# Second-half scores directly behind the first half's sums, and weight forms on another engine, in a two-layer graph network

## The chip, the cores and the metric

The kernel runs on one core of one Trainium2 chip. The metric is the device time of one execution in microseconds (us). The kernel before takes 2780.09 us (median of 3 runs, 2779.88 to 2780.28); the profiled execution below has a span of 2778.7 us. The engines are named as in the profile: PE is TensorE's matmul row and PEld its weight loads, DVE is VectorE, ACT is ScalarE, POOL is GpSimd, SP is the queue that issues most transfers.

## The reference, cut to what matters

Input x holds 128 graphs of 128 nodes with 256 features, adj their 0/1 adjacency. All is float32. Two layers run one after the other, each graph by itself:

```python
# layer 0: attention over the graph's nodes, 8 heads of 32
q, k = heads(src @ Wq + bq), heads(src @ Wk + bk)
attn = softmax(einsum('bhid,bhjd->bhij', q, k) / sqrt(dh))     # over all nodes
for r in range(4):
    v_r = heads(src @ Wv[r] + bv[r])
    out += einsum('bhij,bhjd->bhid', attn * (adj == r), v_r)
x = ln(src + out @ Wo + bo);  x = ln(x + gelu(x @ W1 + b1) @ W2 + b2)
# layer 1: two graph-attention steps, then a feed-forward
h = gat(gat(x, adj, W1, a1), adj, W2, a2)
x = ln(x + h);  x = ln(x + relu(x @ w_ff1 + b) @ w_ff2 + b)
```

adj is 0 or 1, so of the four values v_r only two are ever used. The kernel computes attn on v_0 and the masked attn on v_1 - v_0, adds both, and divides by the plain row sums of the exponentials. A slower pass for other inputs stands behind a test at the end; it does not run here.

## The kernel before, in words

**Tiling.** The 16384 nodes go through in 32 groups of four graphs, 512 rows each (`G = 4`, `T = 512`). A group passes through projections, attention (`attention`), norm, first feed-forward (`first_ffn`), norm, the graph-attention layer (`layer1`), norm, second feed-forward (`second_ffn`), norm and store. Work of three to four groups is woven together.

**Seven products for eight.** The large matrix products are cut into 2 by 2 blocks and done with seven block products instead of eight. That needs sums and differences of the weight blocks, the forms T1 to T4, made once by `combined` (line 182) with four subtractions each for the weights w1, w2 (first feed-forward), wqk, wv (projections), u1, u2 (second feed-forward). On GpSimd these are 24 instructions. It also needs sums of the input blocks, `yS` and `xS`, made by VectorE for every group. A feed-forward (`ffn`, line 394) runs two rounds of the first matrix. In a round, the products into the banks pa (tag "fa"), pe (tag "fe") and `seeded` (tag "fb") follow one another in this order: B11 into pa, which ScalarE copies to `seeded` (line 449 or 483); T3 into pe, copied out to p7; T2 added into `seeded`, copied out to p16; B21 into pa; T1 into `seeded`; T4 into pe; B22 into `seeded`. Each feed-forward block is two products with a 128 by 256 result, which the trace shows as four matmuls. Then come seven products with the second matrix (`product2`, line 420).

**Attention.** A group's four graphs are handled in two halves p = 0, 1 of two graphs. `scores` (line 693) multiplies keys and queries with four 32-row tiles of the array side by side, into four banks (`ps`), and ScalarE takes the exponentials into e. `masked` multiplies e by adj (VectorE, line 725), giving pm. `sums` (line 730) multiplies e and pm by the values into `pav` with four 32-column tiles side by side, and e by ones into `pden`: the plain sums. In groups after the second the plain sums follow pav. ScalarE then reads pden twice (lines 764 and 767: a copy to rd with a running sum, and a relu for the test at the end), VectorE takes the reciprocal and multiplies. `output` projects by Wo.

**Banks.** There are eight: two of tag "s", shared by the transposes, graph-attention products, scores and plain sums, and one each of "qa", "qb", "av", "fa", "fe", "fb". The tile pools make a later user of a bank wait for the readers of the earlier one.

**Order.** The order is written out by hand. Every stage is a generator; `in_order` takes (generator, number of steps) pairs and emits the steps in that order, each engine in its own queue and first in, first out. Step names in the lists: `f1`, `f2` the two feed-forwards, `at` attention, `pr` projections, `l1` the graph-attention layer, `n0` to `n3` the norms, `turned` the transposes of a group with the input sums, `ahead` the same for the second feed-forward's input, `gelu` and `exp` ScalarE's table switches. In the steady loop the second half's scores come four feed-forward blocks behind the first half's sums:

```python
f2, at, (f2, 2), n1, at, f2, at, (f2, 2), lambda: turned(S1, 1), f2, at, (n2, 2), (f2, 2),
```

Here the three first `at` are the first reciprocal, the second reciprocal with the product, and the whole of the second scores.

Of the kernel before, what the change touches and what calls it, by code (L numbers as in the profile page):

```python
# [10 lines left out]
F32 = mybir.dt.float32  # L11
# [13 lines left out]
P = 128  # L25
# [82 lines left out]
def fast_pass(ctx, tc, a, out):  # L108
# [5 lines left out]
    nc = tc.nc  # L114
# [3 lines left out]
    NCH = D // P  # L118
# [14 lines left out]
    ps_s = ctx.enter_context(tc.tile_pool(name="ps_s", bufs=2, space=PSUM))  # L133
    ps_1 = ctx.enter_context(tc.tile_pool(name="ps_1", bufs=1, space=PSUM))
# [46 lines left out]

    def combined(w):
        for o, p, q in ((T3, B22, T1), (T1, T1, B11), (T2, B22, T1), (T4, B21, T2)):
            nc.gpsimd.tensor_sub(w[:, o], w[:, p], w[:, q])


    temp = flat(w1p.tile([P, NF, T], F32, tag="hT", name="temp"))
# [10 lines left out]
    first = dict(g=0, direct=0, xt=load_xT(0))  # L198
    wqk = halved("qk", lambda h: a["L0_gnn_W" + "qk"[h]])
# [3 lines left out]
    wv = halved("v", lambda h: a["L0_gnn_Wv"][h])  # L203
# [14 lines left out]
    w1, b1 = forms("L0_gnn_W1"), k.col("L0_gnn_b1")  # L218
# [4 lines left out]
    w2 = forms("L0_gnn_W2")  # L223
# [469 lines left out]
    def scores(S, p):  # L693

        qT, kT = S["qT"], S["kT"]
        n = f"{S['g']}_{p}"


        banks = ((ps_1, "qa"), (ps_1, "qb"), (ps_s, "s"), (ps_s, "s"))
        pss = [  # L700
            pool.tile([P, 2, NCH, P], F32, tag=t, name=f"ps_{n}_{s}")
            for s, (pool, t) in enumerate(banks if p == 0 and S["g"] > 1 else banks[2:] + banks[:2])
        ]
        for u in range(2):
            bs = slice((2 * p + u) * P, (2 * p + u + 1) * P)
            for c in range(NCH):
                for s in range(HC):
                    rs = slice(s * DH, (s + 1) * DH)
                    nc.tensor.matmul(  # L709
                        pss[s][:, u, c, :], kT[rs, c, bs], qT[rs, c, bs],  # L710
                        start=True, stop=True,
                    )
        S["e", p] = e = w1p.tile([P, HC, 2, NCH, P], F32, tag="e", name="e_" + n)
        for s in range(HC):
            nc.scalar.activation(e[:, s], pss[s], AF.Exp, scale=SCALE)  # L715
            if s == 1:
                yield
# [12 lines left out]
    def sums(S, p):  # L730


        e, pm = S["e", p], S["pm", p]
        n = f"{S['g']}_{p}"
        pden = ps_s.tile([P, 2, NCH, P], F32, tag="s", name="pden_" + n)
        pav = ps_1.tile([P, 2, NCH, P], F32, tag="av", name="pav_" + n)

        def plain():
            for s in range(HC):
                nc.tensor.matmul(  # L740
                    pden[s * DH : (s + 1) * DH], k.ones, e[:, s], start=True, stop=True
                )


        late = S["g"] > 1
        if not late:
            plain()
        for u in range(2):
            v = S["v"][:, 2 * p + u]
            for c in range(NCH):  # L750
                for r, m in enumerate((e, pm)):
                    for s in range(HC):
                        d0 = r * D + c * P + s * DH
                        nc.tensor.matmul(  # L754
                            pav[s * DH : (s + 1) * DH, u, c, :],
                            v[:, d0 : d0 + DH], m[:, s, u, c, :],
                            start=(r == 0), stop=(r == 1),
                        )
        if late:
            plain()  # L760

        g, oT = S["g"], S["oT"]
        rd = w1p.tile([P, 2, NCH, P], F32, tag="rd", name="rd_" + n)
        nc.scalar.activation(
            rd, pden, AF.Identity, accum_out=c_att[:, 1, g, p : p + 1]
        )
        nc.scalar.activation(
            pden, pden, AF.Relu, bias=k.lo, scale=-1.0, accum_out=c_att[:, 0, g, p : p + 1]
        )
        yield  # L770
        nc.vector.reciprocal(rd[:, 0], rd[:, 0])
        yield
        nc.vector.reciprocal(rd[:, 1], rd[:, 1])
        for u in range(2):
            bs = slice((2 * p + u) * P, (2 * p + u + 1) * P)
            nc.vector.tensor_mul(oT[:, :, bs], pav[:, u], rd[:, u])
        yield

    def attention(S):

        n = str(S["g"])
        S["oT"] = oT = w1p.tile([P, NCH, T], F32, tag="oT", name="oT_" + n)

        def output(p):
            po = mm_tile(f"pwo_{n}_{p}")
            for s in range(2):
                b = 2 * p + s
                for c in range(NCH):
                    nc.tensor.matmul(  # L789
                        po[:, s * D : (s + 1) * D], oT[:, c, b * P : (b + 1) * P], wo[:, c, :],  # L790
                        start=(c == 0), stop=(c == NCH - 1),
                    )
            added(S, 0, p, po)

        for p in range(G // 2):
            parts = scores(S, p)
            next(parts)
            if p == 0:
                yield
            next(parts, None)  # L800
            yield
            masked(S, p)
            yield
            yield from sums(S, p)
        for p in range(G // 2):
            output(p)
            yield
# [116 lines left out]
    with tc.manual_schedule(engines={ET.PE, ET.Activation, ET.DVE, ET.SP, ET.Pool}):  # L924
# [6 lines left out]
        S1 = st[1]  # L931
# [4 lines left out]
        def output_bias():  # L936
# [7 lines left out]
            prepared(first)  # L944

        in_order(
            lambda: combined(w1), (pr, 4), (at, 2), (pr, 2), at, (pr, 2), at, lambda: combined(w2), (at, 3), (pr1, 2),
            at, output_bias, at, (pr1, 2), (at, 3), pr1, at, (at1, 2), n0, n0, pr1, at1, lambda: turned(first, 0), (at1, 2),
        )
        f1 = first_ffn(first)  # L950
        prepared(S1)
        st[2] = entered(2)
        pr = projected(st[2])
        in_order(
            gelu, (f1, 4), pr1, f1, f1, at1, at1, f1, pr1, lambda: combined(wqk), lambda: combined(wv), lambda: combined(u1), f1, n0, at1, (f1, 2), n0, f1, at1,
            (f1, 3), gwu, at1, f1, gwu, f1, at1, gwu,
            f1, at1, f1, gwu, at1, lambda: combined(u2), f1, n0_, pr, n0_, (f1, 4), n1_, (pr, 5), lambda: turned(S1, 0),
        )
        for g in range(NG - 1):
            S, S1 = st[g], st[g + 1]  # L960
            more = g + 2 < NG
            f1, f2 = first_ffn(S1), second_ffn(S)
            n1, n2 = norm(S1, 1), norm(S, 2)
            at = n0 = none
            if more:
                S2 = st[g + 2]
                at, n0 = attention(S2), norm(S2, 0)
            ahead = lambda: turned(S, 2)
            ready = (lambda: prepared(st[g + 2])) if more else (lambda: None)
            if g == 0:  # L970
                l1 = layer1(S)
                in_order(
                    f1, n1_, (pr, 2), (f1, 3), lambda: turned(S, 1), (pr, 2), f1, (n0_, 2), f1, l1, f1, (n1_, 2), l1, l1, f1, l1,
                    (f1, 2), (l1, 2), (pr, 2), f1, l1, (pr, 2), f1, pr, l1, f1, l1, f1, (l1, 2), exp, f1, (at, 2), (l1, 2),
                )
            else:
                n3 = norm(st[g - 1], 3)
                in_order(
                    pr, lambda: turned(S1, 0), (pr, 2), *(() if more else (f2_,)), f1, l1, gelu, (pr, 2), f2_, n3, f1, l1, pr,
                    n0_, f1, (pr, 2), (f1, 3), n0_, l1, f1, (pr, 2), l1, f1, n3, (pr, 2), f1, l1, f1, n3, (pr, 2),  # L980
                    (f1, 3), n3, lambda: store(st[g - 1]), f1, (n1_, 2), exp, (at, 2), f1, (l1, 3),
                )
            in_order(
                f1, (pr, 2), l1, f1, (pr, 2), at, f1, (pr, 2), l1, n2, (pr, 2), f1, n2, (pr, 2), f1, (pr, 2), f1, (pr, 2), *((ahead,) if more else ()), at, f1, n1,
                *(() if more else (ahead,)),
            )
            if not more:
                break
            l1 = layer1(S1)
            pr = none  # L990
            if g + 3 < NG:
                st[g + 3] = entered(g + 3)
                pr = projected(st[g + 3])
            in_order(
                f2, at, (f2, 2), n1, at, f2, at, (f2, 2), lambda: turned(S1, 1), f2, at, (n2, 2), (f2, 2),
                at, f2, l1, ready, (f2, 3), l1, f2, at, f2, l1, (f2, 2), at, at, f2, at, n0, l1, f2,
                n0, l1, pr, f2, *((f2,) if g + 3 < NG else ()),
            )
            n0_, n1_, f2_ = n0, n1, f2
        in_order(f2, n1, (f2, 2), lambda: turned(S1, 1))  # L1000
        l1 = layer1(S1)
        in_order(
            (f2, 2), (l1, 3), f2, l1, (f2, 2), (l1, 2), n1, (f2, 2), l1, n1, (f2, 2), (l1, 2), f2, l1, n2, f2, (l1, 3), n2,
            (f2, 3), l1, (f2, 2), l1,
        )
        n2, n3 = norm(S1, 2), norm(S, 3)
# [361 lines left out]
```

## Time and profile before

| what | value |
|---|---|
| time, median of 3 | 2780.09 us |
| period of a group in the steady part (1328.60 to 1412.89) | 84.29 us |
| PE busy from 396 to 1418 us | 1019.6 of 1022 us |
| PE busy from 0 to 140 us | 119.4 of 140 us |
| PE busy from 2660 to 2779 us | 96.2 of 119 us |
| POOL, forms (line 184), start | 24 subtractions: 16 of 1.6 us, 8 of 0.73 us (medians) |
| DVE mask multiply 128x512, median of 256, longest | 0.682 us, 1.765 us |
| mean granted PE clock, 70 to 140 us and 2740 to 2779 us | 0.93 and 0.85 of full speed, about 1.00 elsewhere |

How to read it: in a timeline line the first number is the start in us from the span's start, the second how long the group of instructions lasted, then engine, line, operation, output and inputs, array rows and columns used, shape and how many. A square bracket at the end gives the idle time of the engine before it and what released it. Matmul ends are modelled; the distance from one start to the next, the pitch, is the firm number. In the list of waits the columns are engine and line, what was waited for, total us, how often, and the longest. A PE that is busy 98% of the span leaves 53 us of holes; what a change can close is read in the stage where the hole is.

### The profile page before, as it was taken

The page shows a single profiled execution, that of the slowest core. Times are in us where ns is not written, and L with a number is a line of the kernel's source. Part 1 is how long each engine was busy: PE and PEld are TensorE (multiplying, and loading weights), DVE is VectorE, ACT ScalarE, POOL GpSimd, SP SyncE. Part 2 cuts the span into 40 slices and gives each one's busy share as a digit, 9 for nine tenths or more (in the row PEclk, how much of TensorE's full clock was granted, in tenths as well). Part 3 has the DMA queues.
Part 4 walks back from the last instruction along what each step waited for, and adds up shares of the span by engine and source line. Part 5 has one row for each costly group of instructions (what it writes and reads, how often), then busy time and mean ns, then how long its engine had stood idle before and what let it go on. Part 6 is the DMA issues. An engine that isn't in the chain of part 4 may idle for free.

```text
span 2778.7 us, 54158 instructions
## 1 busy us (share of the span) xinstructions
PE 2725.9 (98%) x21621; PEld 2372.0 (85%) x21621; DVE 2287.3 (82%) x5296; ACT 1613.9 (58%) x3589; POOL 166.7 (6%) x161
## 2 busy tenths in 40 slices
PE   8899999999999999999999999999999999999997
PEld 5688888888888888888888888888888888888876
DVE  5778888888888888888888888888888888888876
ACT  4456556556565566565565565565655665655653
POOL 2200000000000000000000000000000000000000
PEclk9999999999999999999999999999999999999999
DMA  6001100010100101000101000111001110001000
GB/s 177 1 24 32 35 16 28 32 35 32 35 16 24 35 32 35 24 28 24 35 32 35 16 30 29 35 31 35 17 24 35 32 35 27 25 24 35 13 12 17
DMA packets 70234, 86.12 MB, mean 31 GB/s; under 512 B 8428, under 2 KB 48728, under 8 KB 69976
## 3 DMA queue, kind: packets, MB, share of 16 engines
q1 hardware_dynamic: 68872, 82.20, 9.5%
q8 instruction: 172, 2.82, 0.4%
q14 instruction: 86, 0.70, 0.1%
q10 hardware_dynamic: 1104, 0.40, 0.1%
HBM read 65.68 MB, written 16.90 MB: 30 GB/s over the span
## 4 chain that ended last, share of the span: by engine, by line
PE 89%; ACT 4%; DVE 3%; issue 3%; DMA 1%; SPq 0%; ACTq 0%; POOL 0%; DVEq 0%; POOLq 0%
PE po L420 16%; PE ph L411 13%; PE seeded L411 13%; PE seeded L420 12%; PE pqqa L641 4%; PE pwo L789 4%; PE pw L862 4%; PE pvqa L641 4%; PE pav L754 3%; PE pt L300 3%; PE pvqb L641 3%; PE pqqb L641 3%; PE ps L709 2%; PE py L875 2%; PE pg L888 2%
## 5 line engine op out<-in xcount | busy, mean ns | idle before, releaser
L349 ACT ACTIVATE x<-x,sh,rs 128x256 f32<-128x256 f32 x388 | 201.4, 590 | 424.3 <-DVE sh L344 424.3
L335 POOL TENSOR_TENSOR rs<-rs,mhalf 128x4 f32<-128x4 f32 x129 | 133.4, 1034 | 2554.3 <-DVE rs L334 2310.6
L466 DVE TENSOR_TENSOR hT<-seeded,p 128x512 f32<-128x512 f32 x128 | 88.5, 691 | 156.0 <-ACT hT L435 89.5
L411 PE MATMUL seeded<-yS,w_L_gnn_w_ff 128*128 128x256 f32 x768 | 207.3, 392 | 4.9 <-ACT seeded L483 2.2
L411 PE MATMUL seeded<-yS,w_L_gnn_W 128*128 128x256 f32 x768 | 202.0, 386 | 3.2 <-ACT seeded L483 2.2
L411 PE MATMUL ph<-yT,w_L_gnn_w_ff 128*128 128x256 f32 x768 | 200.9, 385 | 0.9 <-ACT yT L303 0.9
L411 PE MATMUL ph<-yT,w_L_gnn_W 128*128 128x256 f32 x768 | 197.4, 379 | 0.4 <-ACT yT L303 0.4
L320 DVE BATCH_NORM_STATS2 st<-x 128x6 f32<-128x256 f32 x512 | 192.1, 417 | 6.7
L411 PEld LDWEIGHTS seeded<-yS,w_L_gnn_w_ff 128*128 128x128 f32 x768 | 138.1, 190 | 63.1 <-ACT seeded L483 28.1
L420 PE MATMUL po<-w_L_gnn_W,hT 128*128 128x128 f32 x1536 | 190.0, 277 | 0.0
L420 PEld LDWEIGHTS po<-w_L_gnn_W,hT 128*128 128x128 f32 x1536 | 183.9, 192 | 6.8
L420 PE MATMUL po<-w_L_gnn_w_ff,hT 128*128 128x128 f32 x1536 | 187.0, 275 | 0.0
L420 PEld LDWEIGHTS po<-w_L_gnn_w_ff,hT 128*128 128x128 f32 x1536 | 184.1, 192 | 3.3
L411 PEld LDWEIGHTS ph<-yT,w_L_gnn_w_ff 128*128 128x128 f32 x768 | 141.1, 190 | 43.3 <-issue 25.2
L411 PEld LDWEIGHTS seeded<-yS,w_L_gnn_W 128*128 128x128 f32 x768 | 138.5, 190 | 40.6 <-DVE hT L466 12.1
L725 DVE TENSOR_TENSOR pm<-e,adj 128x512 f32<-128x512 f32 x256 | 170.2, 725 | 0.0
L411 PEld LDWEIGHTS ph<-yT,w_L_gnn_W 128*128 128x128 f32 x768 | 145.6, 190 | 20.8 <-ACT yT L303 0.7
L435 ACT ACTIVATE hT<-hT,c_L_gnn_b 128x256 f32<-128x256 f32 x256 | 109.5, 497 | 60.2 <-DVE hT L466 58.5
L715 ACT ACTIVATE e<-ps 128x512 f32<-128x512 f32 x256 | 129.8, 589 | 7.5 <-PE ps L709 7.4
L435 ACT ACTIVATE hT<-hT,c_L_gnn_b_ff 128x256 f32<-128x256 f32 x256 | 110.1, 514 | 33.9 <-DVE hT L466 29.6
L834 ACT ACTIVATE gs<-spread,wh 128x128 f32<-128x128 f32 x120 | 38.4, 390 | 156.9 <-DMA spread<-hbm 156.9
L420 PEld LDWEIGHTS seeded<-w_L_gnn_W,hT 128*128 128x128 f32 x1024 | 124.3, 192 | 3.5 <-DVE hT L517 0.2
(196 smaller groups left out, 6522.0 us busy)
## 6 DMA issues: line engine op xcount, KB each, us to landing
xT<-in_xT_dram SPq DMA_DIRECT2D x32, 512.0 KB, 5.8
x<-in_x_dram SPq DMA_DIRECT2D x32, 512.0 KB, 5.1
out_dram<-x SPq DMA_DIRECT2D x31, 512.0 KB, 2.9
spread<-hbm SPq DMA_DIRECT2D x59, 256.0 KB, 3.2
adj<-in_adjT_dram SPq DMA_DIRECT2D x32, 256.0 KB, 4.2
w_L_gnn_W<-in_L_gnn_W_dram SPq DMA_DIRECT2D x8, 256.0 KB, 6.7
w_L_gnn_w_ff<-in_L_gnn_w_ff_dram SPq DMA_DIRECT2D x8, 256.0 KB, 5.0
hbm<-line SPq DMA_DIRECT2D x59, 2.0 KB
```

What stands on the lines that cost most here:

```text
L320: nc.vector.bn_stats(st[:, b % 2, :], S["x"][:, b, :])
L335: nc.gpsimd.tensor_tensor(rs[:, bs], rs[:, bs], k.mhalf[:, bs], op=ALU.pow)
L349: nc.scalar.activation(x[:, b, :], x[:, b, :], AF.Identity, bias=sh[:, b : b + 1], scale=rs[:, b : b + 1],)
L411: nc.tensor.matmul(bank[:, s * TH : (s + 1) * TH], wa[:, form, 0, f * P : (f + 1) * P], m, start=start and s == 0, stop=True, skip_group_c ...
L420: nc.tensor.matmul(bank[:, s * P : (s + 1) * P], m[:, f, s * P : (s + 1) * P], wb_[:, form, f, :], start=start and s + f == 0, stop=True, ...
L435: nc.scalar.activation(o[:, s], o[:, s] if src is None else src[:, s * TH : (s + 1) * TH], func, bias=ba[:, f : f + 1],)
L466: nc.vector.tensor_add(hidden(1, 1, r), halves(seeded), halves(p7))
L641: nc.tensor.matmul(bank[:, s * TH : (s + 1) * TH], *ops, start=start and s == 0, stop=True, skip_group_check=True,)
L715: nc.scalar.activation(e[:, s], pss[s], AF.Exp, scale=SCALE)
L725: nc.vector.tensor_mul(pm[:, s], S["e", p][:, s], S["ad"][:, pair(p), None, :].to_broadcast([P, 2, NCH, P]),)
L789: nc.tensor.matmul(po[:, s * D : (s + 1) * D], oT[:, c, b * P : (b + 1) * P], wo[:, c, :], start=(c == 0), stop=(c == NCH - 1),)
L862: nc.tensor.matmul(pw[:, :NU], yT[:, c, b * P : (b + 1) * P], wu[:, c, :], start=(c == 0), stop=(c == NCH - 1),)
```

## The change

The parts of the diff have three aims.

- `combined` runs on VectorE instead of GpSimd, and its six calls move to other places in the hand-written order of the start, where VectorE is meant to be idle.
- In groups after the second (`late`), the second half's scores stand directly behind the first half's sums, in `attention`, ahead of the reciprocals; their exponentials come in two pairs. The plain sums of the first half take bank "fe" of the feed-forward, so that both banks "s" are free for the scores. The lists of the steady loop are adapted: the scores' step moves from behind the fourth feed-forward block to the front.
- In the tail's list, single feed-forward blocks are put between the steps of the last graph-attention layer.

```diff
     def combined(w):
         for o, p, q in ((T3, B22, T1), (T1, T1, B11), (T2, B22, T1), (T4, B21, T2)):
-            nc.gpsimd.tensor_sub(w[:, o], w[:, p], w[:, q])
+            nc.vector.tensor_sub(w[:, o], w[:, p], w[:, q])
...
         n = f"{S['g']}_{p}"
-        pden = ps_s.tile([P, 2, NCH, P], F32, tag="s", name="pden_" + n)
+
+        pool, tag = (ps_1, "fe") if S["g"] > 1 and p == 0 else (ps_s, "s")
+        pden = pool.tile([P, 2, NCH, P], F32, tag=tag, name="pden_" + n)
...
         for p in range(G // 2):
-            parts = scores(S, p)
-            next(parts)
-            if p == 0:
+            late = S["g"] > 1
+            if p == 0 or not late:
+                parts = scores(S, p)
+                next(parts)
+                if p == 0:
+                    yield
+                next(parts, None)
                 yield
-            next(parts, None)
-            yield
             masked(S, p)
             yield
-            yield from sums(S, p)
+            rest = sums(S, p)
+            next(rest)
+            yield
+            if p == 0 and late:
+                parts = scores(S, 1)
+                next(parts)
+                yield
+                next(parts, None)
+                yield
+            yield from rest
...
         in_order(
-            lambda: combined(w1), (pr, 4), (at, 2), (pr, 2), at, (pr, 2), at, lambda: combined(w2), (at, 3), (pr1, 2),
-            at, output_bias, at, (pr1, 2), (at, 3), pr1, at, (at1, 2), n0, n0, pr1, at1, lambda: turned(first, 0), (at1, 2),
+            (pr, 4), (at, 2), (pr, 2), at, (pr, 2), (at, 4), (pr1, 2),
+            at, output_bias, at, (pr1, 2), (at, 3), pr1, at, (at1, 2), n0, n0, lambda: combined(w1), pr1, at1, lambda: turned(first, 0), (at1, 2),
         )
...
-            gelu, (f1, 4), pr1, f1, f1, at1, at1, f1, pr1, lambda: combined(wqk), lambda: combined(wv), lambda: combined(u1), f1, n0, at1, (f1, 2), n0, f1, at1,
+            gelu, (f1, 4), lambda: combined(w2), pr1, f1, f1, at1, at1, f1, lambda: combined(wqk), pr1, lambda: combined(wv), f1, n0, at1, (f1, 2), n0, f1, at1,
             (f1, 3), gwu, at1, f1, gwu, f1, at1, gwu,
-            f1, at1, f1, gwu, at1, lambda: combined(u2), f1, n0_, pr, n0_, (f1, 4), n1_, (pr, 5), lambda: turned(S1, 0),
+            f1, at1, f1, gwu, at1, f1, n0_, pr, n0_, (f1, 4), n1_, (pr, 5), lambda: turned(S1, 0),
...
-                    f1, n1_, (pr, 2), (f1, 3), lambda: turned(S, 1), (pr, 2), f1, (n0_, 2), f1, l1, f1, (n1_, 2), l1, l1, f1, l1,
+                    f1, n1_, lambda: combined(u1), lambda: combined(u2), (pr, 2), (f1, 3), lambda: turned(S, 1), (pr, 2), f1, (n0_, 2), f1, l1, f1, (n1_, 2), l1, l1, f1, l1,
...
-                f1, (pr, 2), l1, f1, (pr, 2), at, f1, (pr, 2), l1, n2, (pr, 2), f1, n2, (pr, 2), f1, (pr, 2), f1, (pr, 2), *((ahead,) if more else ()), at, f1, n1,
+                f1, (pr, 2), l1, f1, (pr, 2), at, f1, (pr, 2), l1, n2, (pr, 2), f1, n2, (pr, 2), f1, (pr, 2), f1, (pr, 2), *((ahead,) if more else ()), (at, 2), f1, n1,
...
-                f2, at, (f2, 2), n1, at, f2, at, (f2, 2), lambda: turned(S1, 1), f2, at, (n2, 2), (f2, 2),
+                f2, (at, 2), (f2, 2), n1, at, (f2, 3), lambda: turned(S1, 1), f2, at, (n2, 2), (f2, 2),
...
-            (f2, 2), (l1, 3), f2, l1, (f2, 2), (l1, 2), n1, (f2, 2), l1, n1, (f2, 2), (l1, 2), f2, l1, n2, f2, (l1, 3), n2,
+            f2, l1, f2, (l1, 2), f2, l1, (f2, 2), (l1, 2), n1, (f2, 2), l1, n1, f2, l1, f2, l1, f2, l1, n2, f2, (l1, 3), n2,
```

## The prediction

> **What bounds the kernel now.** I read the page first, then the waits of TensorE and its weight loads, then the timelines of the start, of one steady group and of the tail.
>
> ```profile
> PE 2725.9 (98%) x21621; PEld 2372.0 (85%) x21621; DVE 2287.3 (82%) x5296; ACT 1613.9 (58%) x3589; POOL 166.7 (6%) x161
> ```
>
> TensorE (PE) is busy 98% of the span, and the chain that ended last is 89% PE. So a change pays only by closing holes between matmuls or by making a stretch of them take less pitch (start to start). The waits of PE and of its weight loads (PEld; total us, times, longest) say where holes are:
>
> ```profile
> PEld seeded L411 <- ACT seeded L449: 14.7, 31, 0.5
> ...
> PEld pt L300 <- ACT e L715: 12.5, 30, 0.4
> ...
> PE pav L754 <- DVE pm L725: 7.8, 8, 3.3
> ```
>
> The first two come once per group; the third is eight waits, all in the start. One steady group, PE in order of time:
>
> ```profile
> 1433.20 1.04 PE L300 MATMUL pt<-ident,x 128*128 128x128 f32 x8
> 1434.17 0.43 PE L754 MATMUL pav<-e,v 128*32 128x128 f32 x8
> ...
> 1435.94 1.04 PE L740 MATMUL pden<-e,ones 128*32 128x512 f32 x8
> 1436.91 1.13 PE L411 MATMUL ph<-yT,w_L_gnn_w_ff 128*128 128x256 f32 x4
> 1437.88 1.03 PE L411 MATMUL ph<-yS,w_L_gnn_w_ff 128*128 128x256 f32 x4
> 1439.00 1.13 PE L411 MATMUL seeded<-yS,w_L_gnn_w_ff 128*128 128x256 f32 x4
> 1439.96 1.03 PE L411 MATMUL ph<-yT,w_L_gnn_w_ff 128*128 128x256 f32 x4
> 1440.92 1.17 PE L709 MATMUL ps<-qT,kT 32*128 32x128 f32 x32
> 1442.03 1.13 PE L411 MATMUL seeded<-yS,w_L_gnn_w_ff 128*128 128x256 f32 x4
> 1442.99 1.03 PE L411 MATMUL ph<-yT,w_L_gnn_w_ff 128*128 128x256 f32 x4
> 1444.03 1.15 PE L300 MATMUL pt<-ident,x 128*128 128x128 f32 x8
> 1445.02 1.03 PE L411 MATMUL ph<-yT,w_L_gnn_w_ff 128*128 128x256 f32 x4
> ...
> 1447.70 0.43 PE L754 MATMUL pav<-e,v 128*32 128x128 f32 x8
> ```
>
> A feed-forward block of four has a pitch of 0.87 us undisturbed (1445.02 to the next at 1445.88). It is 0.97 next to a change of array shape (128*128, 128*32, 32*128) or just after a hole. From the first pt to the last pav is 14.50 us.
>
> ```profile
> 1437.69 0.65 ACT L767 ACTIVATE pden<-pden,lo 128x512 f32<-128x512 f32 x1
> ...
> 1438.35 0.60 ACT L449 COPY seeded<-ph 128x512 f32<-128x512 f32 x1
> ...
> 1440.22 0.58 ACT L460 COPY p<-seeded 128x512 f32<-128x512 f32 x1 [0.69 <-PE seeded L411]
> ```
>
> ScalarE reads the plain sums (rd, then relu), then copies `seeded`; the block at 1439.00 starts 0.65 after that copy started. That is the hole of 0.26. In the start, VectorE with and without GpSimd beside it:
>
> ```profile
> 54.04 2.69 DVE L725 TENSOR_TENSOR pm<-e,adj 128x512 f32<-128x512 f32 x4
> ```
> ```profile
> 79.19 6.76 DVE L725 TENSOR_TENSOR pm<-e,adj 128x512 f32<-128x512 f32 x4
> ```
> ```profile
> 73.66 13.43 POOL L184 TENSOR_TENSOR w_L_gnn_w_ff<-w_L_gnn_w_ff 128x512 f32<-128x512 f32 x8
> ```
>
> The same four multiplies cost 0.67 us each alone and 1.69 each beside L184.
>
> [...] here the mean granted clock is 0.93 between 70 and 140 us, the blocks there have twice the pitch (1.69 at 89.13), and 0.85 after 2740.
>
> **Part 1, forms on VectorE.** GpSimd loses 24 subtractions (16 of 1.6 us, 8 of 0.73: 31.4 us). VectorE gets 16 of about 0.67 and 8 of about 0.40, 14 us, by its own rows of those shapes. PE and VectorE gain at four places in the start, measured by one sums block, 2.74 in the steady group (1434.17 to 1436.91):
> - 23.39 to 27.97 is 4.58: minus 1.8. Multiplies from 20.79 then end at 23.5, before pav needs them.
> - 35.28 to 38.67 is 3.39: minus 0.6.
> - 54.77 to 58.44 is 3.67. Its multiplies were not stretched, and `combined(w1)` now stands just ahead of them. VectorE had holes of 1.13 and 2.40 there, and w1 needs 2.75: minus 0.3.
> - 76.46 to 89.13 is 12.67. Replaying VectorE: `combined(w2)` (2.75) fits 61.6 to 64.4, where it waited 2.79; `combined(wqk)` (1.6) fits 68.7 to 71.7; `combined(wv)` delays the h subtractions from 72.10 to 73.8; these end at 75.8, two scale multiplies at 77.0, the mask multiplies at 79.6. pav wants the last at 77.6, so a hole of 2.0 remains: 2.74 + 2.0 = 4.8, minus 7.9. With it goes the half clock on the next block (1.69 for 0.87): minus 0.8.
> - `combined(u1)` and `(u2)` need 5.4 ahead of the add at 124.93, which has 5.36 of idle time before it; behind it are ScalarE's gelu and the copy wh, for which PE waits at 129.88: plus 0.3.
>
> Sum: minus 11.1. The two bounds: minus 7, if VectorE queues more or the half clock stays; minus 12 with no hole left.
>
> **Part 2, second scores behind the first sums, 30 groups.** Removed: one change of shape into ps and one out (0.10 before 1440.92, 0.10 behind), and the hole before pt (0.17 and its 0.10 after), since the exponentials then free the banks early. Added: the exponentials (0.48 each in a run of four) stand in ScalarE's queue ahead of `seeded` (two) and of p7 and p16 (two). pden in bank fe adds a wait of the T3 block for relu, done at 1438.34, long before T3. Bank s is free, since yT was read by 1435.3. Replay:
> - pden 1435.94, ps 1436.91 (I take the change 128*32 to 32*128 at the price of one to 128*128; the trace never shows this pair clear of other things but at 27.55 to 27.97, 0.42, as to 128*128 at 38.26), B11 1438.02, T3 1438.99, T2 ready 1439.86.
> - ScalarE: relu to 1438.35, two exponentials to 1439.31, copy starts 1439.31, so T2 starts at 1439.96 (hole 0.10). B21 1440.92, T1 ready 1441.79.
> - ScalarE: two exponentials to 1440.76, p7 to 1441.24, p16 starts 1441.24; T1 may start 1441.89 (hole 0.10). Then T4 1442.85, pt 1443.72. Queued behind p16 are the four normalizations of x that pt reads (0.50 each, done 1443.8; pt wants the fourth at 1444.05), then the activations freeing bank fa (started by 1444.1, wanted at 1444.59). Then 1445.45, 1446.32, pav 1447.28. The mask multiplies end at 1447.0, before pav needs them.
>
> 14.08 for 14.50: minus 0.42 a group, 30 times, minus 12.6. Bounds: holes at T2 and T1[...] gone altogether, minus 0.8 a group; 0.1 us more per step in ScalarE's queue, five steps, plus 0.1.
>
> **Part 3, tail.** pw is taken one block earlier, where yT is not ready until 2699.4 (a new hole of 0.7 for the 0.29 removed); a block now stands between py pairs, where PE waited 1.86 at 2716.22. The two replayed: minus 0.9; bounds minus 2.5 and plus 1 (the half-clock window near 2739 may fall otherwise).
>
> Sum: 2780.1 - 11.1 - 12.6 - 0.9 = 2755.5; I say 2756.5, since a replay misses waits more often than it invents them.
>
> **The rivals.**
> 1. ScalarE takes it back: the exponentials ahead of `seeded` and p16 cost what the change of shape saves. For: the hole at 1439.00 is ScalarE's already. Against: 1.8 us of idle time before rd. Steady gain 0.05 a group: 2780 - 11 - 2 - 1 = 2766.5.
> 2. The change of shape is worth more and the new holes vanish: 0.75 a group: 2780 - 11 - 22 - 1 = 2746.
> 3. Slower. ScalarE's delay runs on through x, pt and the activations: each group loses two new holes of 0.5, plus 30 us, and VectorE's added 14 us keeps the start's gain at 7: 2780 - 7 + 30 = 2803; half of that is 2788. Against: x is normalized 0.25 ahead of need in the replay, and VectorE is not on the path there.
> 4. The start gives nothing, steady as forecast: 2780 - 2 - 12.6 - 1 = 2764.5. Against: the 1.69 is plainly L184's.
>
> **How the numbers follow.** Forecast 0.56, rival 1 0.20, rival 2 0.12, rival 3 0.05, rival 4 0.07. 0.2% is 5.6 us, so only rival 3 and the edge of rival 1 are not faster: faster 0.93, same 0.03, slower 0.04. The range leaves out rival 3 and the far ends of 1 and 2: 2746 to 2769.
>
> **What would show it.** No L184 on GpSimd; all mask multiplies of the start near 0.67; a sums block of about 5 us instead of 12.67 near 74, and no half clock there. In each group ps directly behind pden, holes of 0.1 before T2 and T1, none before pt, period 83.9 for 84.3 (1328.60 to 1412.89). The forecast is wrong if the period stays at 84.3 or grows, with p16 or x named as releaser, or if pm still holds pav for over 3 us.

## The result, and the profile after

The changed kernel takes 2761.53 us (median of 4 runs, 2759.64 to 2762.1), the kernel before 2779.99 us beside it (2779.53 to 2780.28): 18.5 us less, a ratio of 0.9933, 95% interval 0.9915 to 0.995. The forecast was 2756.5 us in a range of 2746 to 2769. The profiled execution has a span of 2759.6 us for 2778.7. From the page of the kernel after, the busy time of the engines:

```profile
PE 2717.9 (98%) x21621; PEld 2374.0 (86%) x21621; DVE 2285.9 (83%) x5320; ACT 1608.6 (58%) x3589; POOL 135.9 (5%) x137
```

GpSimd has lost 24 instructions and 30.8 us. VectorE has gained 24, some 15 us, and is nevertheless busy 1.4 us less, because its other instructions are no longer stretched: the mask multiplies of the start alone lose 11 us. From the waits of the kernel after (engine and line, what was waited for, total us, times, longest):

```profile
PEld seeded L411 <- ACT p L460: 13.9, 35, 1.4
PEld seeded L411 <- ACT seeded L449: 11.7, 34, 0.4
...
PE pav L756 <- DVE pm L725: 0.8, 4, 0.2
```

`pav` waits 0.8 us for the mask multiplies where it waited 7.8. The weight loads wait for ScalarE's copies twice a group now, at `seeded` (L449) and at p16 (L460), and the wait of pt for the exponentials is no longer in the list.

Where the 19.2 us of the two traces went is read from three common points. The first two, before:

```profile
169.72 0.43 PE L754 MATMUL pav<-e,v 128*32 128x128 f32 x8
...
2674.83 1.95 PE L420 MATMUL po<-w_L_gnn_W,hT 128*128 128x128 f32 x16
```

And after:

```profile
160.06 0.43 PE L756 MATMUL pav<-e,v 128*32 128x128 f32 x8
...
2656.51 1.95 PE L420 MATMUL po<-w_L_gnn_W,hT 128*128 128x128 f32 x16
```

The first `pav` of the third group starts 9.66 us earlier: that is the start. The product with the hidden rows that opens the last stretch starts 18.32 us earlier: 8.66 us more are the steady part. `pflag`, the last product, is at 2771.54 and 2752.30, an offset of 19.24: 0.92 us are the tail.

One steady group, PE in order of time, after:

```profile
1419.22 1.04 PE L300 MATMUL pt<-ident,x 128*128 128x128 f32 x8
...
1421.96 1.04 PE L742 MATMUL pden<-e,ones 128*32 128x512 f32 x8
1422.93 1.17 PE L709 MATMUL ps<-qT,kT 32*128 32x128 f32 x32
...
1425.98 1.13 PE L411 MATMUL seeded<-yS,w_L_gnn_w_ff 128*128 128x256 f32 x4
...
1427.95 1.13 PE L411 MATMUL seeded<-yS,w_L_gnn_w_ff 128*128 128x256 f32 x4
...
1429.78 1.04 PE L300 MATMUL pt<-ident,x 128*128 128x128 f32 x8
1430.66 1.11 PE L411 MATMUL ph<-yT,w_L_gnn_w_ff 128*128 128x256 f32 x4
1431.61 1.03 PE L411 MATMUL seeded<-yS,w_L_gnn_w_ff 128*128 128x256 f32 x4
...
1433.43 0.42 PE L756 MATMUL pav<-e,v 128*32 128x128 f32 x8
```

The scores `ps` stand directly behind `pden`, 0.97 after its start. A duration of 1.13 for 1.03 marks, among others, the blocks in front of which PE stood for a moment: the T2 block at 1425.98 and the T1 block at 1427.95. The first block of the second round, at 1430.66, has 1.11, which was not forecast. It starts 0.88 behind pt, so PE hardly stood in front of it, but the next block follows only 0.95 later. From pt to the last pav it is 14.21 us for 14.50, and the period of a group is 84.00 us for 84.29. ScalarE in the same stretch:

```profile
1424.36 1.08 ACT L715 ACTIVATE e<-ps 128x512 f32<-128x512 f32 x2
1425.32 0.62 ACT L449 COPY seeded<-ph 128x512 f32<-128x512 f32 x1
...
1427.26 0.64 ACT L460 COPY p<-seeded 128x512 f32<-128x512 f32 x1
...
1429.71 0.88 ACT L435 ACTIVATE hT<-ph,c_L_gnn_b_ff 128x256 f32<-128x256 f32 x2
```

The copies start at 1425.32 and 1427.26, and the products behind them 0.66 and 0.69 later: the two holes. The last line is the pair of activations that frees bank fa; it ends at 1430.59, and the block that takes that bank starts at 1430.66. The weight loads of this block and of the next one (PEld; the first is released by these activations):

```profile
1430.64 0.73 PEld L411 LDWEIGHTS ph<-yT,w_L_gnn_w_ff 128*128 128x128 f32 x4
1431.39 0.84 PEld L411 LDWEIGHTS seeded<-yS,w_L_gnn_w_ff 128*128 128x128 f32 x4
```

The next block has its first weights 0.22 ahead of its start, this one 0.02.

In the start, VectorE's mask multiplies of the stretch that cost most before, after:

```profile
75.90 2.49 DVE L725 TENSOR_TENSOR pm<-e,adj 128x512 f32<-128x512 f32 x4
```

Four in 2.49 us where they took 6.76; no GpSimd form is beside them.

### The profile page after: what moved, and what is told of

It is laid out like the page before. It is cut to its first block, busy times and chain, and to the rows that moved or that the text cites. A ratio compares the mean times of both kernels' runs of the same rounds, so it can differ in the third digit from the quotient of the medians.

```text
span 2759.6 us, 54205 instructions
## 1 busy us (share of the span) xinstructions
PE 2717.9 (98%) x21621; PEld 2374.0 (86%) x21621; DVE 2285.9 (83%) x5320; ACT 1608.6 (58%) x3589; POOL 135.9 (5%) x137
## 4 chain that ended last, share of the span: by engine, by line
PE 94%; DVE 3%; ACT 2%; issue 0%; POOL 0%; ACTq 0%; POOLq 0%; DVEq 0%
PE po L420 16%; PE ph L411 15%; PE seeded L411 13%; PE seeded L420 12%; PE pav L756 4%; PE pwo L791 4%; PE pw L875 4%; PE pqqa L641 4%; PE pvqa L641 4%; PE pt L300 3%; PE pvqb L641 3%; PE pqqb L641 3%; PE ps L709 3%; PE py L888 2%; PE pden L742 2%; PE pg L901 2%
## 5 line engine op out<-in xcount | busy, mean ns | idle before, releaser
L725 DVE TENSOR_TENSOR pm<-e,adj 128x512 f32<-128x512 f32 x256 | 159.1, 683 | 0.0
```

What stands on the lines that cost most here:

```text
L725: nc.vector.tensor_mul(pm[:, s], S["e", p][:, s], S["ad"][:, pair(p), None, :].to_broadcast([P, 2, NCH, P]),)
```

## The experiments

Times are medians with the kernel before on the same chip beside them: 2780.37 us for the first four below, 2781.43 for the next four, 2781.03 for the last two.

**The forms alone.** The changed `combined` and its six new places, nothing else of the change:

```diff
-            nc.gpsimd.tensor_sub(w[:, o], w[:, p], w[:, q])
+            nc.vector.tensor_sub(w[:, o], w[:, p], w[:, q])
...
-            lambda: combined(w1), (pr, 4), (at, 2), (pr, 2), at, (pr, 2), at, lambda: combined(w2), (at, 3), (pr1, 2),
+            (pr, 4), (at, 2), (pr, 2), at, (pr, 2), (at, 4), (pr1, 2),
...
```

> The kernel before with part 1 alone: forms on VectorE, at the new places; attention and tail as before. Theory[...]: the start gains about 9.7 as between the two profiles, 11.4 if no half-clock window falls into the start: 2768.5 to 2770.5, period still 84.29, first sums of the third group at about 160 instead of 169.7. Rival (the start's gain comes from the new attention order): under 3 us, 2777 or more.

2771.36 us, ratio 0.9967 (0.9955 to 0.9979): minus 9.0. From `pden` to the next pav a steady group takes 11.76 us on the mean of 26 groups, as before: the steady part is untouched. The first pav of the third group is at 160.43.

**The second scores alone.** The hunks of `sums` and `attention` and the two steady lists:

```diff
+        pool, tag = (ps_1, "fe") if S["g"] > 1 and p == 0 else (ps_s, "s")
+        pden = pool.tile([P, 2, NCH, P], F32, tag=tag, name="pden_" + n)
...
-                f2, at, (f2, 2), n1, at, f2, at, (f2, 2), lambda: turned(S1, 1), f2, at, (n2, 2), (f2, 2),
+                f2, (at, 2), (f2, 2), n1, at, (f2, 3), lambda: turned(S1, 1), f2, at, (n2, 2), (f2, 2),
```

> The kernel before with part 2 alone: second scores behind the first sums, plain sums in bank fe. Theory: 30 groups at 0.285 each, period 84.01, minus 8.6: about 2771.4; the start unchanged (first sums of the third group at 169.7). Rival (a shorter start lets the steady part run differently): period stays near 84.3, 2779.

2772.34 us, ratio 0.997 (0.9959 to 0.9981): minus 8.0. The same stretch of a steady group takes 11.47 us, as in the changed kernel. The two parts add up: 9.0 and 8.0 are 17.0 of the 18.5, and the tail and the scatter hold the rest.

**The engine undone: the forms at their new places, on GpSimd.**

```diff
-            nc.vector.tensor_sub(w[:, o], w[:, p], w[:, q])
+            nc.gpsimd.tensor_sub(w[:, o], w[:, p], w[:, q])
```

> The changed kernel with the forms back on GpSimd, at the new places of the order. Theory[...]: GpSimd's work now meets other mask multiplies. Those of the first group run free (0.67 each); those of the second group's first half, beside w1 and w2, are stretched to about 1.5 each: plus 3, 2764 to 2765. Rival 'engine': GpSimd's forms are too slow wherever they stand, so nearly all 9.7 us come back: 2771. Rival 'place alone': nothing is lost, 2761.5.

2772.24 us, ratio 0.9966 (0.9954 to 0.9979): 10.7 above the changed kernel, and in the trace 10.54 (the first pav of the third group at 170.60 for 160.06). The theory that the new places lose only about 3 us on GpSimd was wrong; that the engine decides was right. Up to 3.4 us of the 10.54, an estimate from the 1.7 that such a window costs in the next run but one, are two half-clock windows (stretches at a granted clock of 0.50) that the changed kernel's trace lacks: the granted clock is 0.83 between 60 and 70 us and between 120 and 130 us here, and 1.00 there. GpSimd and VectorE in this run:

```profile
49.97 12.27 POOL L184 TENSOR_TENSOR w_L_gnn_W<-w_L_gnn_W 128x512 f32<-128x512 f32 x8
```
```profile
53.99 5.71 DVE L725 TENSOR_TENSOR pm<-e,adj 128x512 f32<-128x512 f32 x4
59.62 1.49 DVE L389 TENSOR_TENSOR yS<-yT 128x256 f32<-128x256 f32 x1
```

A form that GpSimd makes is not done when VectorE is idle but whenever GpSimd comes to it: the forms of w1 and w2 run together for 12.27 us and stretch the masks of the group and then the input sums `yS`, 1.49 us for the 0.42 of such an operation alone. The same happens at 111.11 with u1 and u2: PE then stands 1.57 us for a `yS`, and `pt` 1.12 for x behind it.

**The places undone: the forms on VectorE, at their old places.** The edit is that of one line in the kernel before:

```diff
-            nc.gpsimd.tensor_sub(w[:, o], w[:, p], w[:, q])
+            nc.vector.tensor_sub(w[:, o], w[:, p], w[:, q])
```

> The kernel before with the forms on VectorE at the old places. Theory: the multiplies are unstretched (0.67), but VectorE's queue now waits for the weights' transfers (w1 at 18.6, w2 near 30) with adds, reciprocals and masks queued behind, and u1 stands ahead of the last masks: holes of 3, 4 to 5 and 4.5 us in PE take back most of 11: about 2777 (2774 to 2781). Rival (the engine is all that matters): 2769 as with the new places.

2784.19 us, ratio 1.0012 (1.0006 to 1.0019): 3.8 slower than before, where a gain had been expected. The mask multiplies are not stretched (2.48 to 2.78 us for four), but the subtractions now stand at the head of a first-in first-out queue that others need:

```profile
29.54 2.87 DVE L184 TENSOR_TENSOR w_L_gnn_W<-w_L_gnn_W 128x512 f32<-128x512 f32 x4 [4.24 <-DMA w_L_gnn_W<-in_L_gnn_W_dram]
```

VectorE sits 4.24 us until the transfer of w2 lands, with the reciprocals and the masks of the second half behind it; these masks start at 36.21 for 30.73 before. So the engine alone costs 3.8, the places alone give about nothing (the run before this one, 2772.24, is as fast as the scores alone, 2772.34), and the two together give 9.0.

**The changed kernel once more.** No edit.

> The changed kernel once more, as the measure for the other runs of this chip: 2761.5 (2759.5 to 2762.5). Theory on its spread: half-clock windows of 3.41 us that fall into busy stretches cost 1.7 us each, so single runs differ by that step. Rival: the spread is the same as with all kernels and has nothing to do with windows.

2760.15 us (2759.29 to 2764.18, 5 runs), ratio 0.9928 (0.9914 to 0.9941). Its trace differs from the first one in one place of the start and in one of the tail. The projection behind the first wait for an exponential, in the first trace of the changed kernel:

```profile
28.96 5.40 PE L579 MATMUL pq<-xT,w_qk 128*128 128x512 f32 x8 [1.65 <-ACT e L715]
```

And in this trace:

```profile
29.50 3.70 PE L579 MATMUL pq<-xT,w_qk 128*128 128x512 f32 x8 [1.65 <-ACT e L715]
```

The same eight products behind the same wait take 5.40 or 3.70 us: in the first trace the granted clock is 0.50 from 29.18 to 32.59 us (0.87 between 30 and 40 us), in this one 1.00 from 20 to 110 us. One half-clock window costs 1.70 us here and falls or does not fall with the execution. In the tail, the first trace has a clock of 0.89 and 0.77 in the two stretches of 5 us from 2715 to 2725, this one 1.00; the blocks are at full speed:

```profile
2719.26 1.13 PE L411 MATMUL ph<-yT,w_L_gnn_w_ff 128*128 128x256 f32 x4 [0.43 <-ACT yT L303]
2720.23 1.03 PE L411 MATMUL ph<-yS,w_L_gnn_w_ff 128*128 128x256 f32 x4
```

From the product that opens the last stretch to `pflag` it is 94.81 us here for 95.79 in the first trace of the same program.

**The hole before that projection filled.** One and a half extra products on the identity behind the seventh attention step, into bank `seeded`; the second restarts the sum in half of that bank, so that the seed of the first feed-forward's first round is probably left out there.

```diff
+        def busy():
+            nc.tensor.matmul(seeded, k.ident, over(k.ident), start=True, stop=True)
+            nc.tensor.matmul(seeded[:, : 2 * P], k.ident, over(k.ident, 2), start=True, stop=True)
...
-            (pr, 4), (at, 2), (pr, 2), at, (pr, 2), (at, 4), (pr1, 2),
+            (pr, 4), (at, 2), (pr, 2), at, (pr, 2), (at, 4), busy, (pr1, 2),
```

> The changed kernel with two extra matmuls (512 and 256 wide, their result is never used) in TensorE's hole between the first group's second scores and the next group's projections (27.3 to 28.9). Theory: the half-clock window that stood at about 29 in the profile, with the projections at 5.40 us instead of 3.70, is set by that hole; filled, the projections take 3.70 and the median falls by up to 1.7, about 2760. Rival: the window comes from something else[...], projections still 5.40 in the profile, 2761.5 or 0.2 more.

2761.32 us, ratio 0.9927 (0.9913 to 0.994): no gain that shows. The hole is down to 0.16 us and the projection takes 3.70, but a half-clock stretch stands later:

```profile
53.85 1.93 PE L742 MATMUL pden<-e,ones 128*32 128x512 f32 x8
```

That block takes 1.06 us in the first trace of the changed kernel; the clock is 0.66 between 50 and 60 us in this run. With one trace each this does not show that filling the hole is useless, only that it does not keep such windows out of the start.

**The plain sums back in bank "s".** In the changed kernel:

```diff
-        pool, tag = (ps_1, "fe") if S["g"] > 1 and p == 0 else (ps_s, "s")
+        pool, tag = ps_s, "s"
```

> The changed kernel with the first half's plain sums in a bank s again, as before the change, and the scores still directly behind them. Theory: one of the two banks s that the scores need is then held until ScalarE has read the plain sums twice, 1.4 us after ps could start; 30 groups times 1.4 to 1.5: plus 43, about 2805, with a hole before ps in each group. Rival (the bank is only tidiness, the other banks give slack): 2761.5, no hole.

2804.59 us, ratio 1.0083 (1.0065 to 1.0101): 43 above the changed kernel and 23 above the kernel before. PE at the scores:

```profile
1446.28 1.17 PE L709 MATMUL ps<-qT,kT 32*128 32x128 f32 x30 [1.11 <-ACT pden L769]
```

Two of the 32 products go out, then the rest waits 1.11 us for ScalarE's relu to let go of the second bank "s", in every group; from `pden` to pav it is 12.90 us for 11.47. The feed-forward bank is not an extra: without it the move loses.

**The exponentials behind the copies.** In the changed kernel the scores' products stay directly behind the sums, but the exponentials come after the copy to `seeded` (first pair) and after the copy to p16 (second pair):

```diff
+        if p and S["g"] > 1:
+            yield
         S["e", p] = e = w1p.tile([P, HC, 2, NCH, P], F32, tag="e", name="e_" + n)
...
-                f2, (at, 2), (f2, 2), n1, at, (f2, 3), lambda: turned(S1, 1), f2, at, (n2, 2), (f2, 2),
+                f2, at, (f2, 2), (at, 2), n1, at, (f2, 3), lambda: turned(S1, 1), f2, at, (n2, 2), (f2, 2),
```

> The changed kernel with the second half's exponentials moved in ScalarE's queue: the first two behind the copy of seeded, the last two behind the copy p16; TensorE's order is the same. Theory A (rival 1 of the prediction, ScalarE takes back part of the gain): the holes before T2 and T1 vanish[...], minus 0.2 to 0.3 a group, about 2754. Theory B (the holes are the chain product, copy, next product itself: 1.13 + 0.09 + 0.65 = 1.87 for two blocks of 1.83, so the exponentials cost next to nothing): minus 0.1 a group at most, 2758.5 to 2762.

2785.64 us, ratio 1.0016 (1.0009 to 1.0022): slower than both kernels, which neither theory had. Means of 26 groups: the T2 block comes 0.863 after the T3 block (0.985 in the changed kernel), so that hole is gone. But the copy is done only just in time, the weights are loaded 0.04 ahead of the product, and the block behind T2 comes 0.927 after it for the 0.86 of an undisturbed block:

```profile
1438.17 0.73 PEld L411 LDWEIGHTS seeded<-yS,w_L_gnn_w_ff 128*128 128x128 f32 x4 [0.20 <-ACT seeded L449]
```

The T1 block still comes 1.006 after the B21 block (1.000). Its copy to p16 is still queued here, behind the first pair of exponentials and the copy to p7, so this run does not test T1's hole. The traces allow an estimate. In the kernel before, where ScalarE was idle in front of this copy, it starts 0.26 after the B21 block and lasts 0.58; in the changed kernel it is 0.31 and 0.64, and the product follows 0.05 after its end. An idle ScalarE would then give 0.89: of the hole of 0.14 about 0.03 is the chain product, copy, product itself, and the rest is ScalarE's queue. What was gained is lost many times over at the transposes:

```profile
1442.58 0.33 PE L300 MATMUL pt<-ident,x 128*128 128x128 f32 x1 [0.16 <-ACT x L349]
```

The second pair now stands ahead of the four normalizations of x: they start at 1440.90 and last 2.11, and pt takes each of them as it comes. From the first pt to the block behind it it is 1.82 us for 0.87. This is the prediction's rival 3 in small: x had 0.25 us to spare in the replay, and two exponentials of 0.48 are more than that.

**The tail alone.** The kernel before with the changed tail list.

```diff
-            (f2, 2), (l1, 3), f2, l1, (f2, 2), (l1, 2), n1, (f2, 2), l1, n1, (f2, 2), (l1, 2), f2, l1, n2, f2, (l1, 3), n2,
+            f2, l1, f2, (l1, 2), f2, l1, (f2, 2), (l1, 2), n1, (f2, 2), l1, n1, f2, l1, f2, l1, f2, l1, n2, f2, (l1, 3), n2,
```

> The kernel before with the changed tail list alone. Theory A (the tail is independent of what goes before it): from the last product of the last attention to the last sum of the test the trace is 0.9 us shorter than in the kernel before, as it is in the changed kernel, and the time is 2779.2 us, which can't be told from 2780.1 us. Theory B (the tail's gain in the changed kernel comes from the earlier scores or another phase of the half clock near the end): no difference, or up to 1.7 us either way.

2780.29 us, ratio 0.9996 (0.9987 to 1.0005): no difference that the times can tell. In the trace the tail is 94.86 us (2675.77 to 2770.63) for 96.71 before and 95.79 in the changed kernel, so twice what was expected. The respaced stretch itself, up to the first product with the hidden rows of the last feed-forward, is 44.77 us, 44.75 in the changed kernel and 44.99 before: minus 0.22 to 0.24. The rest lies after it, where the order is the same in all of them. The first two feed-forward blocks behind the last transposes, before:

```profile
2739.09 1.85 PE L411 MATMUL ph<-yT,w_L_gnn_w_ff 128*128 128x256 f32 x4 [0.43 <-ACT yT L303]
2740.73 1.91 PE L411 MATMUL ph<-yS,w_L_gnn_w_ff 128*128 128x256 f32 x4
```

The changed kernel, from its last transposes on:

```profile
2718.77 1.82 PE L300 MATMUL pt<-ident,x 128*128 128x128 f32 x6 [0.16 <-ACT x L349]
2720.61 1.95 PE L411 MATMUL ph<-yT,w_L_gnn_w_ff 128*128 128x256 f32 x4
```

And with the tail alone:

```profile
2739.75 1.13 PE L411 MATMUL ph<-yT,w_L_gnn_w_ff 128*128 128x256 f32 x4 [0.43 <-ACT yT L303]
2740.72 1.03 PE L411 MATMUL ph<-yS,w_L_gnn_w_ff 128*128 128x256 f32 x4
```

One half-clock window stands on two blocks before (1.85 and 1.91) and on the transposes and one block in the changed kernel, where part of it falls on PE's waits for x. With the tail alone there is none near: the granted clock is 1.00 from 2735 to 2745 us. From the first of these transposes to the fourth block behind them it is 7.05 us before, 6.44 after, and 5.47 here and in the second trace of the changed kernel, which has no window there either. That second trace has the same tail as this run, 94.81 and 94.86 us: the difference of 0.9 between this run and the first trace of the changed kernel is the window's.

**The later half of the tail alone.** The changed kernel with the front of its tail list as before:

```diff
-            f2, l1, f2, (l1, 2), f2, l1, (f2, 2), (l1, 2), n1, (f2, 2), l1, n1, f2, l1, f2, l1, f2, l1, n2, f2, (l1, 3), n2,
+            (f2, 2), (l1, 3), f2, l1, (f2, 2), (l1, 2), n1, (f2, 2), l1, n1, f2, l1, f2, l1, f2, l1, n2, f2, (l1, 3), n2,
```

> The changed kernel with the front of the tail's list put back as before (two feed-forward blocks, three steps of the last graph-attention layer), and the later respacing kept. Theory A (the two halves of the tail's respacing act apart: taking pw one block early costs 0.43 us, because pw then waits for yT, and a block between the py pairs saves 0.68 us plus what is shared): the stretch from the first block of the tail to its fourth is back at 6.75 us for 7.18, the rest keeps 8.44 us, the whole is 0.4 us faster than the changed kernel: about 2761.1 us, which the times can't tell from it, but the trace can. Theory B (the early pw is what makes the later saving possible, since everything behind it on VectorE starts earlier): the front is back at 6.75 us, but the later stretch goes back towards 9.1 us, and the whole is 0.2 us slower than the changed kernel.

2761.06 us, ratio 0.9928 (0.9915 to 0.9942). The respaced stretch is 44.33 us for 44.75: 6.76 from its B21 block to its T4 block (7.18 in the changed kernel), and 8.43 from the block at 2693.06 to the product with the hidden rows (8.44). The two halves act apart: the front costs 0.42, the later half gains 0.66. This is the version that the traces point to; 0.4 us can't be told from the changed kernel in the times.

## Why the prediction was right or wrong

**Part 1, minus 11.1: right, stretch by stretch.** The first block of sums is 2.74 us for 4.58 (forecast minus 1.8, measured 1.84), the second 2.74 for 3.39 (0.6, measured 0.65), the third 3.46 for 3.67 (0.3, measured 0.21), the fourth 4.68 for 12.67 (7.9, measured 7.99: 1.94 above the undisturbed 2.74 where a hole of 2.0 was forecast); the block behind it has a pitch of 0.97 for 1.69 (0.8, measured 0.72); the wait for wh is 1.69 for 1.58 (plus 0.3, measured 0.11). They sum to 11.3. The trace shows 9.66, because the window at 28.96 takes 1.70 back; 11.36 without it. That window was not in the forecast. The runs with the forms alone, with the engine undone and with the places undone show that the cause is the one seen in the trace of before: VectorE's multiplies and sums beside GpSimd's subtractions (0.42 becomes 1.49 with the engine undone, as 0.67 became 1.69 before). How the two engines slow each other was not shown.

**Part 2, minus 12.6: the mechanism right, the gain a third smaller than forecast.** The steady part gained 8.66, and the scores alone 8.0. Scores directly behind `pden`, holes at T2 and T1, none before pt, x in time: all as forecast. The replay gave 11.34 us from `pden` to pav; the mean of 26 groups is 11.47, and 0.13 in each of 30 groups is 3.9 us. The term that failed is the activations "freeing bank fa (started by 1444.1, wanted at 1444.59)": here the bank came free when its reader ended, not when it started, and the block's weights, which wait for the same bank, are normally loaded ahead of it. The pair ends 0.07 us before the block starts at 1430.66, the weights are loaded at 1430.64 where the next block has them 0.22 early, and the next block comes 0.95 later for the 0.86 of the replay: 0.09 of the 0.13. The other 0.04 lies in T2 (0.985 for 0.97) and T1 (1.000 for 0.97). That the late weights make the 0.09 is read from the trace; no run takes it away, but the T2 block of the run with the exponentials behind the copies shows the same thing a second time (loaded 0.04 ahead, next block 0.927 later). So most of the 0.10 after the old hole before pt, which the replay took away, did not go: it moved one block on. The chance given to rival 1 was for more than this: a gain of 0.29 a group is nearer to the forecast of 0.42 than to the rival's 0.05.

**Part 3, minus 0.9: the number met, for the wrong reason.** The trace gives 0.92, but the respacing gave 0.24 of it. The front's sum was met (0.42 lost; forecast 0.7 of new hole for 0.29), its terms were not: the wait of 0.29 was not removed, for PE waits 0.30 for wh in front of `pr` instead, and the new hole is smaller, about 0.5 from the pitches of the block and of pw around it (1.02 and 2.09, for 0.87 and 1.75 where nothing is waited for). The gain of the later half was forecast too large: the wait of 1.86 before the second py pair is gone, but the first pair, now one block earlier, waits longer for its scaled rows. PE before:

```profile
2713.23 1.14 PE L875 MATMUL py<-wh,gs 128*128 128x258 f32 x4 [0.44 <-DVE gs L851]
2716.22 1.14 PE L875 MATMUL py<-wh,gs 128*128 128x258 f32 x4 [1.86 <-ACT yh L878]
```

And in the changed kernel:

```profile
2695.35 1.14 PE L888 MATMUL py<-wh,gs 128*128 128x258 f32 x4 [1.50 <-DVE gs L864]
...
2699.40 1.16 PE L828 MATMUL pr<-ident,yh 128*128 128x128 f32 x8 [0.32 <-ACT yh L891]
```

The waits of 0.44 and 1.86 have become 1.50 and 0.32: most of the time is still spent waiting for VectorE and ScalarE, in other places. Of the other 0.68, about 0.6 is the half-clock window near the end (7.05 against 6.44 us above), which the prediction named as a bound and not as a part. That the sum came to 0.9 is luck.

**The sum.** Forecast 2755.5 by the parts and 2756.5 on record, measured 2761.53. Of the 6.0 us above the sum of the parts 3.9 are part 2 and 1.7 the window in the start. Rival 1 was partly right in kind: the holes at T2 and T1 cost a little more than forecast, but far from the whole gain. Rival 2 was not the case, for those holes did not vanish. Rival 3 was not the case either, but its mechanism lies one list entry away, as the run with the exponentials behind the copies shows, and rival 4 is refuted by the forms alone.

## What to carry to other kernels

Moving work to an idle engine and moving it to an idle time are two edits that may each be worth nothing or less, and pay together: here GpSimd, otherwise idle, slowed VectorE's multiplies from 0.67 to 1.69 us, and VectorE's queue stood 4.24 us for a transfer that had not landed. When products are moved ahead of what frees their banks, look for a bank whose readers end early enough and price its alternatives in the same replay, and reckon a bank as free from the end of its last reader, in time for the weight load ahead of the product (here the reader ended 0.07 us before the block, whose weights were loaded 0.02 ahead where the next block has 0.22). Before a gain of a microsecond is credited to an edit, compare the stretch that was edited and not the whole, for something else may have moved.

## What the runs showed that was not expected

- Where the half clock falls is not settled by the program alone. The same program had a window at 29 us in one trace and none in another (5.40 and 3.70 us for eight products), and in five traces with the same end of the tail (before, both of the changed kernel, and the two runs on the tail) the window near it lay on two blocks in one, on transposes and the block behind them in two, and was absent in two. The window at 29.18 us and the ones in the tails of the changed kernel's first trace and of the kernel before (from 2718.88 and 2739.35 us) lasted 3.41 us each, at a granted clock of 0.50. Half of that, 1.70 us, is what the first of them cost, where PE was busy throughout (0.98 in the tail, where part of it fell on waits). The half clock of the kernel before from 80.37 to 90.61 us lasted 10.24 us, three times as long. What sets the lengths and the places was not shown.
- VectorE's shorter sums were stretched beside GpSimd too: `yS` of 256 columns went from 0.42 to 1.49 us beside subtractions of about 1.5 us, a larger factor than the masks' 0.67 to 1.69.
- With one block of four between them, a product, its copy by ScalarE and a product into the copied bank leave no slack: by the estimate above about 0.89 us with ScalarE idle, for a pitch of 0.86, and 1.00 measured where the copy is queued behind others.
- A block can start on time and still cost 0.06 to 0.09 us, where its bank comes free so late that its weights are loaded with it and not ahead of it (pitches of 0.927 and 0.95 for 0.86).
